# Last step of a two-layer graph kernel as seven half products on one Trainium2 core

## The chip, the core and the metric

The kernel runs on one core of one Trainium2 chip. The core has five engines that run side by side and meet at semaphores: TensorE (matrix products into PSUM; PE in the profile, with its weight loads as PEld), VectorE (DVE), ScalarE (ACT), GpSimd (POOL) and SyncE (SP), whose queue issues almost all transfers of this kernel, in order. The metric is the device time of the whole program in microseconds (us); lower is better. All data is float32.

## What is computed

There are 16 batches of 1024 nodes with 256 channels, and one adjacency matrix of 1024 x 1024 for all of them. Layer 0 is an attention over the nodes whose queries come from a product with a weighted adjacency; layer 1 is a graph convolution in two steps with a residual. Each layer ends in a LayerNorm over the 256 channels. The change concerns layer 1:

```python
def _graph_conv(x, adj, w_loop, w_neigh, b):
    loop = jnp.einsum('bnd,dh->bnh', x, w_loop)
    neigh = jnp.einsum('nm,bmh->bnh', adj, jnp.einsum('bnd,dh->bnh', x, w_neigh))
    return loop + neigh + b
h = jax.nn.relu(_graph_conv(x, adj, w1_loop, w1_neigh, b1))   # 256 -> 128
h = jax.nn.relu(_graph_conv(h, adj, w2_loop, w2_neigh, b2))   # 128 -> 256
return (x + h) * 0.5
...
x = _layernorm(x + _L1_gnn_ref(x, adj, ...), axis=-1)
```

With u = adj h1 (128 wide, one row per node), the second step ends in h2 = u w2_neigh + h1 w2_loop + b2. That is one product of [u, h1] (1024 x 256) with the two stacked weight matrices (256 x 256). Since LayerNorm undoes a common factor, the kernel scales w2 and b2 by 1/3 and adds relu(h2) to the layer's input x1 directly.

## The kernel before

**Batches overlap.** The loop over b in `run` works on four batches at once: the attention of batch b, the queries, keys and values of batch b + 1, the graph convolution's second half for batch b - 2 joined with the first half for batch b - 1, and the LayerNorm and output of batch b - 3. From batch 2 on, `c1`, `c2` and `c3` are the convolutions of b - 1, b - 2 and b - 3. The order in which the engines get their work is written out by hand (`tc.manual_schedule()`), so an engine does what the program issues for it, in the program's order, and each engine waits by itself for what it needs.

**One batch in order** (batches 2 to 14, the branch `elif more`):

- Scores of the first head pair (L692), exponentials on ScalarE (L697, L699), sums of the exponentials on VectorE (`collect`, L711 and L713, then the block transpose L718 and the reduction L721 in `partial`).
- Meanwhile the 256-channel sums of the next batch's x on ScalarE (`NodeSums`, L276), which write x in place.
- Products of exponentials and values (L734) for two units, each drained by a transpose on VectorE (L745); between them the transposes of the next x (L228).
- Sums for keys and values of the next batch (`KeysValues.sums`, L413 to L421, VectorE).
- `c1.inner()`: t = x1 w1_neigh (L847), copied by ScalarE (L850).
- `both.left(nc.gpsimd)`: four sums of blocks of t and h1 on GpSimd, the tiles R (L1052 to L1055).
- `both.run(...)`: the joined product with the adjacency, for t of batch b - 1 and h1 of batch b - 2 together: seven products of quarters instead of eight (Strassen-Winograd), issued as 1, 2, 6, 7, 5, 4, 3 (L1061), with the loop term of the first step (L854) at the start and ahead of product 3. It uses three PSUM banks called first, third and second, which ScalarE copies out (L1077, L1083, L1087, L1090). Its results are h1 of batch b - 1 (L860) and u of batch b - 2 (upper half on VectorE, L1094; lower half on GpSimd, L1095).
- Between the products other work is issued through the dictionary handed to `run`: the sums S of blocks of the next x for its queries (`q.left`, GpSimd, L596 to L599) after product 1; `att.add` (denominators by a small product L754, then L760 to L767 on VectorE) after product 2; `likeness` (two ScalarE activations, L550 and L551) and `c3.moments` (statistics L300 and L301 on VectorE, variance plus epsilon L305 there, power -1/2 on GpSimd L306) after product 6; `likeness` again after 7; `weigh_first` (L556, L609 to L612, VectorE) after 5; `c3.finish` (scaling L312 on VectorE and the output store L945 on SP) after 4.
- `c2.last()`: the last step of batch b - 2, 16 products 256 wide (L916 with w2_neigh, L918 with w2_loop) into two large PSUM tiles; for each tile VectorE adds b2 (L923), and then takes the maximum with 0 and adds x1 (L926).
- `c1.turn_blocks()` (L876 and stores of h1), scores and outputs of the second head pair, and `weigh_second`.
- The queries' seven products for the next batch, in four steps (`q.pair`, `q.step`, L637), `att.add` for the second pair, the mean and squares of the first LayerNorm, `q.load_para`, `kv.load` (weight sums kept in DRAM), loads of the next x in two layouts (L96, L108), then keys and values by seven products (L434 and L438), the variance with its power on GpSimd (L351), and the first LayerNorm's scaling (L356), transposes (L228) and stores (L364).

Batch 15 (the branch `else`) has no next batch: only `both.left`, `both.run` with `att.add` and the first LayerNorm woven in, `c1.turn(0)` (transposes on TensorE, L893), `c2.last()`, `c1.turn(1)`. After the loop come the convolutions that are left.

**Buffers.** Most tiles of 128 x 1024 come from one pool of 31 buffers (`row_tile`); a new tile waits for the last reader of the tile that had its buffer. PSUM has three large tiles ("big") and two single banks ("bank").

Of the kernel before, what the change touches and what calls it, by code (L numbers as in the profile page):

```python
# [10 lines left out]
F32 = mybir.dt.float32  # L11
# [7 lines left out]
def kernel(  # L19
# [108 lines left out]


    kv_sums = dram.tile([P, N], F32, tag="kv_sums", name="kv_sums", bufs=1)  # L130

    def sum_kv_weights():
        t = row_tile("kv_sums")
# [10 lines left out]
    def load_weights():  # L144
        nc.sync.dma_start(out=w1l_sb, in_=w1_loop.rearrange("(cc p) f -> p cc f", p=P))
        nc.sync.dma_start(out=w1n_sb, in_=w1_neigh.rearrange("(cc p) f -> p cc f", p=P))
        nc.sync.dma_start(out=w2l_sb, in_=w2_loop)
        nc.sync.dma_start(out=w2n_sb, in_=w2_neigh)
        nc.sync.dma_start(out=b1_sb, in_=b1.rearrange("(p o) -> p o", o=1))
        nc.sync.dma_start(out=b2_sb, in_=b2.rearrange("(o f) -> o f", o=1).to_broadcast([P, C]))  # L150

        for w in (w2l_sb, w2n_sb, b2_sb):
            nc.gpsimd.tensor_scalar_mul(w, w, 1.0 / 3.0)
        for w in (w1l_sb, w1n_sb):
            nc.gpsimd.tensor_scalar_mul(w, w, LIFT)

    ident = const.tile([P, P], F32, name="ident")
    make_identity(nc, ident)
# [164 lines left out]
    class BlockedNorm:  # L323
# [23 lines left out]
        def variance(self):  # L347
            self.rstd = small.tile([P, NB], F32, tag="rstd1", name=f"rstd1_{self.name}", bufs=2)
            nc.vector.tensor_scalar(self.rstd, fold_sums(self.part, f"sum2_{self.name}", half_psum), 1.0 / C, EPS,  # L349
                                    op0=ALU.mult, op1=ALU.add)  # L350
            nc.gpsimd.tensor_tensor(self.rstd, self.rstd, neg_half, ALU.pow)  # L351

# [479 lines left out]
    class GraphConv:  # L832
# [95 lines left out]
        def last(self):  # L928
# [6 lines left out]
                filled.append(p2)  # L935
            return filled

        def moments(self):
            self.mv = small.tile([P, NT, 2], F32, tag="mv", name=f"mv_{self.b}", bufs=2)
            statistics(self.mv, self.x, range(NT), f"g{self.b}")  # L940
            self.rstd = reciprocal_deviation(self.mv, f"g{self.b}", EPS2)

        def finish(self, dst):
# [86 lines left out]
    class Joined:  # L1030
# [24 lines left out]
            eng.tensor_sub(s34[:, 1], t1[1], s12[:, 1])  # L1055
            self.x = {1: t1[0], 2: t1[1], 3: s34[:, 1], 4: h1[1], 5: s12[:, 0], 6: s12[:, 1], 7: s34[:, 0]}

        def product(self, n, dst, start=False, again=False):
            rows = self.far[{1: "00", 2: "10", 3: "11", 4: 4, 5: 1, 6: 2, 7: 3}[n]]
            for k in range(TJ):  # L1060
                nc.tensor.matmul(dst, self.x[n][:, k, :], of_rows(rows, k),  # L1061
                                 start=(start and k == 0), stop=(k == TJ - 1), skip_group_check=again)

        def run(self, between=None):
            c1, c2, b = self.c1, self.c2, self.b
            between = between or {}

            def turn_to(n):
                for f in between.get(n, ()):
# [9 lines left out]
            self.product(2, third)  # L1079
            nc.vector.tensor_add(p1, p1, third)  # L1080
            turn_to(2)
            self.product(6, first, again=True)
            nc.scalar.copy(u1, first)  # L1083
            c1.relu(0, p1)
# [9 lines left out]
            nc.vector.tensor_add(c2.uT[:, 0:FB], u1, second)  # L1094
            nc.gpsimd.tensor_add(c2.uT[:, FB:N], u3, p7)  # L1095
            turn_to(4)
            c1.loop(first, 1, again=True)
            self.product(3, first, again=True)
            c1.relu(1, first)
            turn_to(3)  # L1100

    def run():
# [58 lines left out]
        for b in range(B):  # L1161
# [72 lines left out]
            elif more:  # L1234
# [10 lines left out]
                    ready["xT"] = channel_major(blocked, f"xT_{b + 1}")  # L1245

                two_units(0, before_second=next_xT)
                kv = KeysValues(b + 1, ready["xT"])
                kv.sums()
                both.fetch(2, 3)  # L1250
# [3 lines left out]
                for t in (0, TJ):  # L1254
# [13 lines left out]
                order = (1, TJ + 1, 2, TJ + 2, 3, TJ + 3)  # L1268
# [54 lines left out]
            elif more:  # L1323
                q.pair(2)
                q.step(0)
                q.step(1, lambda: att.add(*((2, 3) if both else (3,))), 5)
                q.pair(3)
                q.step(2, norm.mean)
# [12 lines left out]
            else:  # L1341
# [96 lines left out]
```

## Time and profile before

| what | value |
|---|---|
| median of three runs | 2139.09 us (2138.91 to 2139.37) |
| the profiled execution's own time | 2138.39 us |
| its span, first to last instruction | 2136.6 us |
| granted TensorE clock | 0.998 |
| one batch in the middle, t_ps to t_ps | 131.5 us |
| last step in such a batch, L916 and L918 | 6.9 us |
| VectorE, ScalarE, GpSimd busy | 89%, 49%, 16% |
| transfers | 341 MB, 159 GB/s over the span from HBM and to it |

In the timeline each row has the start in the span, the duration, the engine, the line, the operation, output and input with their shapes, and how many instructions were merged; in brackets stands how long the engine was idle before it, and what released it. The chain of waits lists start, duration, engine and line. A float32 product shows as two records, each with its own weight load. Durations on TensorE overlap, since products are pipelined; the distance from one start to the next is what a product costs.

### The profile page before, as it was taken

The page shows a single profiled execution, that of the slowest core. Times are in us where ns is not written, and L with a number is a line of the kernel's source. Part 1 is how long each engine was busy: PE and PEld are TensorE (multiplying, and loading weights), DVE is VectorE, ACT ScalarE, POOL GpSimd, SP SyncE. Part 2 cuts the span into 40 slices and gives each one's busy share as a digit, 9 for nine tenths or more (in the row PEclk, how much of TensorE's full clock was granted, in tenths as well). Part 3 has the DMA queues.
Part 4 walks back from the last instruction along what each step waited for, and adds up shares of the span by engine and source line. Part 5 has one row for each costly group of instructions (what it writes and reads, how often), then busy time and mean ns, then how long its engine had stood idle before and what let it go on. Part 6 is the DMA issues. An engine that isn't in the chain of part 4 may idle for free.

```text
span 2136.6 us, 24125 instructions
## 1 busy us (share of the span) xinstructions
PE 2124.6 (99%) x8374; PEld 1028.2 (48%) x8374; DVE 1896.7 (89%) x2373; ACT 1048.5 (49%) x1498; POOL 345.7 (16%) x191
## 2 busy tenths in 40 slices
PE   9999999999999999999999999999999999999998
PEld 5344544544445455454454444544445444544454
DVE  6899988989898898988989989899998999989964
ACT  5745545555355462545625555355554445545412
POOL 1010120121302113030130301303012130121021
PEclk9999999999999999999999999999999999999999
DMA  9295666736676275763747638466473666734544
GB/s 236 98 171 196 133 214 145 187 121 119 216 156 218 82 137 197 158 217 105 145 168 153 217 122 154 149 148 217 132 178 124 138 217 146 181 117 97 162 158 157
DMA packets 611409, 341.09 MB, mean 160 GB/s; under 512 B 491728, under 2 KB 556624, under 8 KB 611280
## 3 DMA queue, kind: packets, MB, share of 16 engines
q1 hardware_dynamic: 611008, 339.21, 60.9%
q8 instruction: 68, 1.11, 0.2%
q14 instruction: 61, 0.50, 0.1%
q10 hardware_dynamic: 272, 0.26, 0.0%
HBM read 289.54 MB, written 49.87 MB: 159 GB/s over the span
## 4 chain that ended last, share of the span: by engine, by line
PE 98%; DVE 1%; issue 0%; ACT 0%; POOL 0%; POOLq 0%; DVEq 0%
PE s L692 21%; PE av L734 20%; PE hu_ps L1061 17%; PE g_ps L637 15%; PE v_ps L438 5%; PE k_ps L434 5%; PE t_ps L847 3%; PE g_ps L564 3%; PE h_ps L916 2%; PE h_ps L918 2%; PE hu_ps L854 2%; PE h_ps L869 1%; PE u_ps L898 1%; PE den_ps L754 0%; DVE wg L556 0%
## 5 line engine op out<-in xcount | busy, mean ns | idle before, releaser
L713 DVE TENSOR_TENSOR acc<-acc,pr 128x1024 f32<-128x1024 f32 x384 | 473.2, 1232 | 36.7 <-DVE acc L713 0.9
L699 ACT ACTIVATE pr<-s 128x1024 f32<-128x1024 f32 x392 | 390.7, 1115 | 142.2 <-PE s L692 142.2
L692 PE MATMUL s<-qT,kT 64*128 64x512 f32 x2048 | 449.7, 593 | 0.0
L734 PE MATMUL av<-pr,v 128*64 128x512 f32 x2048 | 447.0, 594 | 0.0
L692 PEld LDWEIGHTS s<-qT,kT 64*128 64x128 f32 x2048 | 196.3, 187 | 235.5 <-issue 187.3
L734 PEld LDWEIGHTS av<-pr,v 128*64 128x64 f32 x2048 | 144.0, 137 | 297.3 <-issue 272.6
L351 POOL TENSOR_TENSOR rstd<-rstd,neg_half 128x32 f32<-128x32 f32 x16 | 100.2, 6260 | 1116.1 <-DVE rstd L349 1116.1
L1061 PE MATMUL hu_ps<-adj,R 128*128 128x512 f32 x480 | 211.8, 594 | 0.0
L550 ACT ACTIVATE wg<-c_row,c_sums 128x1024 f32<-128x1024 f32 x120 | 137.1, 1142 | 86.5 <-DVE den_part L721 65.8
L556 DVE SCALAR_TENSOR_TENSOR wg<-wg,adj 128x1024 f32<-128x1024 f32 x128 | 150.1, 1210 | 5.0 <-ACT wg L551 5.0
L697 ACT ACTIVATE pr<-s 128x512 f32<-128x512 f32 x240 | 142.4, 702 | 0.3 <-PE s L692 0.3
L1061 PEld LDWEIGHTS hu_ps<-adj,R 128*128 128x128 f32 x480 | 90.1, 190 | 108.1 <-issue 105.0
L551 ACT ACTIVATE wg<-wg 128x1024 f32<-128x1024 f32 x128 | 135.3, 1057 | 4.1
L637 PE MATMUL g_ps<-T,S 128*128 128x512 f32 x224 | 116.5, 602 | 0.2 <-DVE T L611 0.2
L637 PE MATMUL g_ps<-wg,S 128*128 128x512 f32 x224 | 115.5, 597 | 0.0
L850 ACT COPY t<-t_ps 128x1024 f32<-128x1024 f32 x16 | 16.2, 1013 | 189.4 <-PE t_ps L847 189.4
L637 PE MATMUL g_ps<-wg,x 128*128 128x512 f32 x224 | 109.0, 599 | 0.0
L1061 PE MATMUL hu_ps<-adj,t 128*128 128x512 f32 x240 | 105.7, 592 | 0.0
L646 ACT COPY P<-g_ps 128x512 f32<-128x512 f32 x14 | 8.2, 586 | 183.9 <-PE g_ps L637 106.6
L923 DVE TENSOR_TENSOR z<-h_ps,b_sb 128x1024 f32<-128x1024 f32 x30 | 36.7, 1224 | 59.4 <-PE h_ps L918 59.4
L1052 POOL TENSOR_TENSOR R<-h 128x512 f32<-128x512 f32 x14 | 28.2, 2012 | 358.2 <-DMA adj<-adjT 241.5
L711 DVE TENSOR_TENSOR acc<-pr,pr 128x1024 f32<-128x1024 f32 x64 | 76.9, 1201 | 6.2 <-ACT pr L699 6.2
(210 smaller groups left out, 3131.3 us busy)
## 6 DMA issues: line engine op xcount, KB each, us to landing
adj<-adjT SPq DMA_DIRECT2D x210, 512.0 KB
adj<-in_adj_dram SPq DMA_DIRECT2D x128, 512.0 KB
para<-in_L_gnn_para_dram SPq DMA_DIRECT2D x32, 512.0 KB
xB_a<-in_x_dram SPq DMA_DIRECT2D x128, 128.0 KB
x1d<-xB_a SPq DMA_DIRECT2D x128, 128.0 KB
x<-x1d SPq DMA_DIRECT2D x16, 1024.0 KB
xB<-in_x_dram SPq DMA_DIRECT2D x120, 128.0 KB
x<-in_x_dram SPq DMA_DIRECT2D x15, 1024.0 KB
```

What stands on the lines that cost most here:

```text
L434: nc.tensor.matmul(dst, self.a[0][n], self.w[n], start=not again, stop=True, skip_group_check=again)
L438: nc.tensor.matmul(dst[:, ts(t, P)], self.w[n][:, ts(t, P)], self.a[1][n], start=not again and t == 0, stop=True, skip_group_check=again o ...
L550: nc.scalar.activation(wg, self.c_row, AF.Abs, bias=self.c_col[:, t:t + 1], scale=-1.0)
L551: nc.scalar.activation(wg, wg, AF.Tanh, scale=-0.5 / C)
L556: nc.vector.scalar_tensor_tensor(wg, wg, 1.0, self.adj.pop(t), op0=ALU.add, op1=ALU.mult)
L637: nc.tensor.matmul(self.p[n], x_n[:, k, :], w_n, start=(k == 0), stop=(k == TJ - 1))
L692: nc.tensor.matmul(halves[s], self.kT[rows, pair, ts(mt, P)], self.qT[rows, pair, ts(j, FB)], start=True, stop=True)
L697: nc.scalar.activation(pr[:, ts(s, FB)], halves[s], AF.Exp)
L699: nc.scalar.activation(pr, ps, AF.Exp)
L713: nc.vector.tensor_add(self.acc, self.acc, prs[mt])
L734: nc.tensor.matmul(pav[s * HD:(s + 1) * HD, :], self.v[:, mt, pair * P + s * HD:pair * P + (s + 1) * HD], prs[mt][:, ts(s, FB)], start=(mt ...
L1061: nc.tensor.matmul(dst, self.x[n][:, k, :], of_rows(rows, k), start=(start and k == 0), stop=(k == TJ - 1), skip_group_check=again)
```

## The change

The last step of batch b - 2 is written as seven products of 128 x 128 blocks: [u, h1] is cut into u and h1 by columns and into upper and lower half by rows, the stacked weights into four 128 x 128 blocks. Sums of the weight blocks and the difference of the two halves of b2 are made once, on GpSimd, and kept in DRAM. In each batch they are fetched into a row buffer, and sums of blocks of u and h1 are made (one on GpSimd, three on VectorE). ScalarE writes the bias into two of the joined product's banks before the new products add to them. The joined product's product 3 is cut in two: the order on TensorE is loop term, half of product 3, parts 1, 2, 6, 5, 7, the other half of product 3, parts 4 and 3. This holds for batches 2 to 15 of the loop; the convolutions after the loop keep the old last step.

Beside that, the work woven in between the joined products is placed anew. `q.left` (S) and the statistics of batch b - 3 now stand ahead of the keys' and values' sums; the two `likeness` calls, `att.add`, the deviation and `weigh_first` stand after products 1 and 2. The last LayerNorm's scaling goes to ScalarE (`finish_aside`, as it was used after the loop before), after step 0 of the queries' products, and its store to the same place. In batch 15 the variance uses a single bank, and the first LayerNorm's scaling and transposes stand after the new block sums.

```diff
+    w2_sums = dram.tile([P, 5 * P], F32, tag="w2_sums", name="w2_sums", bufs=1)
@@ load_weights
+        t = row_tile("w2_sums")
+        (b11, b12), (b21, b22) = ((w[:, ts(0, P)], w[:, ts(1, P)]) for w in (w2n_sb, w2l_sb))
+        t1, t2, t3, t4, b2_step = (t[:, ts(n, P)] for n in range(5))
+        nc.gpsimd.tensor_sub(t1, b12, b11)
...
+        nc.gpsimd.tensor_sub(b2_step, b2_sb[:, ts(1, P)], b2_sb[:, ts(0, P)])
+        nc.sync.dma_start(out=w2_sums, in_=t[:, 0:5 * P])
@@ GraphConv
+        def load_sums(self):
+            self.w2 = row_tile(f"w2_sums_{self.b}")
+            nc.sync.dma_start(out=self.w2[:, 0:5 * P], in_=w2_sums)
+            self.b2_step = self.w2[:, ts(4, P)]
+
+        def block_sums(self, base, lower):
...
+            lower()
+            nc.gpsimd.tensor_add(s1, self.h1T[:, FB:N], self.low)
+            base()
+            nc.vector.tensor_sub(s2, s1, self.up)
+            nc.vector.tensor_sub(s4, self.h1T[:, 0:FB], s2)
+            nc.vector.tensor_sub(s3, self.up, self.low)
...
+        def seventh_part(self, n, dst, start=False):
+            a, w = self.factors[n]
+            for t in range(TJ):
+                first = start and t == 0
+                nc.tensor.matmul(dst[:, ts(t, P)], a[:, ts(t, P)], w, start=first, stop=True, skip_group_check=not first)
+
+        def settle(self, i, j, src):
+            rows = self.x[:, ts(i, TJ), ts(j, P)]
+            nc.vector.scalar_tensor_tensor(rows, src.rearrange("p (t c) -> p t c", c=P), 0.0, rows,
+                                           op0=ALU.max, op1=ALU.add)
+
+        def last_products(self, a, c):
...
+            self.seventh_part(1, a)
+            nc.scalar.copy(p1, a)
+            self.seventh_part(2, d, start=True)
+            nc.vector.tensor_add(p1, p1, d)
+            self.settle(0, 0, p1)
+            self.seventh_part(6, a)
+            nc.scalar.copy(u2, a)
+            self.seventh_part(5, c)
+            self.seventh_part(7, a)
+            nc.scalar.copy(u3, a)
+            nc.vector.tensor_add(u3, u3, c)
+            self.settle(1, 1, u3)
+
+            def rest():
+                self.seventh_part(4, a)
+                self.settle(1, 0, a)
+                self.seventh_part(3, c)
+                nc.vector.tensor_add(u2, u2, c)
+                self.settle(0, 1, u2)
...
@@ Joined.run
             turn_to(2)
+            if last:
+                bias(third, b2_sb[:, ts(0, P)])
+                c2.load_sums()
...
+            c2.block_sums(add_upper, add_lower)
+            bias(second, c2.b2_step)
             turn_to(4)
             c1.loop(first, 1, again=True)
-            self.product(3, first, again=True)
+            self.product(3, first, again=True, steps=range(0, TJ // 2))
+            rest = c2.last_products(third, second)
+            self.product(3, first, again=True, steps=range(TJ // 2, TJ))
             c1.relu(1, first)
+            rest()
@@ run, batches 2 to 14
                 two_units(0, before_second=next_xT)
+                q.left(nc.gpsimd)
+                if c3:
+                    c3.statistics()
                 kv = KeysValues(b + 1, ready["xT"])
                 kv.sums()
...
-                both.run({1: (lambda: q.left(nc.gpsimd),),
-                          2: (lambda: att.add(0, 1),),
-                          6: (lambda: q.likeness(0), lambda: c3 and c3.moments()),
-                          7: (lambda: q.likeness(TJ),),
-                          5: (weigh_first,),
-                          4: (lambda: c3 and c3.finish(out[b - 3]),)})
-                c2.last()
+                both.run({1: (lambda: q.likeness(0),),
+                          2: (lambda: att.add(0, 1), lambda: q.likeness(TJ), lambda: c3 and c3.deviation(), weigh_first)},
+                         last=True)
...
                 q.step(0)
+                if c3:
+                    c3.finish_aside(out[b - 3])
                 q.step(1, lambda: att.add(*((2, 3) if both else (3,))), 5)
@@ run, batch 15
-                          5: (norm.variance,), 4: (norm.scale, norm.spread)})
+                          5: (lambda: norm.variance(bank_psum),), 4: (norm.scale, norm.spread)}, last=True)
                 c1.turn(0)
-                c2.last()
                 c1.turn(1)
```

More of the change, by code (lines that the diff above doesn't have):

```diff
@@ L155, in load_weights @@
             nc.gpsimd.tensor_scalar_mul(w, w, LIFT)
+        t = row_tile("w2_sums")
+        (b11, b12), (b21, b22) = ((w[:, ts(0, P)], w[:, ts(1, P)]) for w in (w2n_sb, w2l_sb))
+        t1, t2, t3, t4, b2_step = (t[:, ts(n, P)] for n in range(5))
+        nc.gpsimd.tensor_sub(t1, b12, b11)
+        nc.gpsimd.tensor_sub(t2, b22, t1)
+        nc.gpsimd.tensor_sub(t3, b22, b12)
+        nc.gpsimd.tensor_sub(t4, b21, t2)
+        nc.gpsimd.tensor_sub(b2_step, b2_sb[:, ts(1, P)], b2_sb[:, ts(0, P)])
+        nc.sync.dma_start(out=w2_sums, in_=t[:, 0:5 * P])
     ident = const.tile([P, P], F32, name="ident")
@@ L345, in sum_squares, with variance @@
             join(self.part)
-        def variance(self):
+        def variance(self, psum_tile=half_psum):
             self.rstd = small.tile([P, NB], F32, tag="rstd1", name=f"rstd1_{self.name}", bufs=2)
-            nc.vector.tensor_scalar(self.rstd, fold_sums(self.part, f"sum2_{self.name}", half_psum), 1.0 / C, EPS,
+            nc.vector.tensor_scalar(self.rstd, fold_sums(self.part, f"sum2_{self.name}", psum_tile), 1.0 / C, EPS,
                                     op0=ALU.mult, op1=ALU.add)
@@ L936, in last @@
             return filled
+        def load_sums(self):
[3 more added lines that the diff above has]
+        def block_sums(self, base, lower):
+            s12, s34 = (row_tile(f"last_{self.b}_{k}") for k in range(2))
+            self.low, self.up = self.uT[:, FB:N], self.uT[:, 0:FB]
+            s1, s2, s3, s4 = s12[:, 0:FB], s12[:, FB:N], s34[:, 0:FB], s34[:, FB:N]
+            lower()
[4 more added lines that the diff above has]
+            nc.vector.tensor_sub(s3, self.up, self.low)
+            t1, t2, t3, t4 = (self.w2[:, ts(n, P)] for n in range(4))
+            self.factors = {1: (self.up, w2n_sb[:, ts(0, P)]), 2: (self.h1T[:, 0:FB], w2l_sb[:, ts(0, P)]),
+                            3: (s4, w2l_sb[:, ts(1, P)]), 4: (self.h1T[:, FB:N], t4), 5: (s1, t1), 6: (s2, t2), 7: (s3, t3)}
@@ new lines, in last_products @@
+        def last_products(self, a, c):
+            name = f"h2_{self.b}"
+            d = bank_psum(f"{name}_ps")
+            snaps = [row_tile(f"{name}_{k}") for k in range(2)]
+            p1, u2, u3 = snaps[0][:, 0:FB], snaps[0][:, FB:N], snaps[1][:, 0:FB]
+            self.seventh_part(1, a)
[16 more added lines that the diff above has]
+                self.settle(0, 1, u2)
+            return rest
@@ L938, in moments, with statistics, deviation @@
         def moments(self):
+            self.statistics()
+            self.deviation()
+        def statistics(self):
             self.mv = small.tile([P, NT, 2], F32, tag="mv", name=f"mv_{self.b}", bufs=2)
             statistics(self.mv, self.x, range(NT), f"g{self.b}")
+        def deviation(self):
             self.rstd = reciprocal_deviation(self.mv, f"g{self.b}", EPS2)
@@ L1056, in left, with product, run, bias @@
             self.x = {1: t1[0], 2: t1[1], 3: s34[:, 1], 4: h1[1], 5: s12[:, 0], 6: s12[:, 1], 7: s34[:, 0]}
-        def product(self, n, dst, start=False, again=False):
+        def product(self, n, dst, start=False, again=False, steps=range(TJ)):
             rows = self.far[{1: "00", 2: "10", 3: "11", 4: 4, 5: 1, 6: 2, 7: 3}[n]]
-            for k in range(TJ):
+            for k in steps:
                 nc.tensor.matmul(dst, self.x[n][:, k, :], of_rows(rows, k),
                                  start=(start and k == 0), stop=(k == TJ - 1), skip_group_check=again)
-        def run(self, between=None):
+        def run(self, between=None, last=False):
             c1, c2, b = self.c1, self.c2, self.b
             between = between or {}
+            def bias(bank, row):
+                nc.scalar.copy(bank.rearrange("p (t c) -> p t c", c=P), row.unsqueeze(1).to_broadcast([P, TJ, P]))
             def turn_to(n):
@@ L1093, in run @@
             c2.uT = row_tile(f"uT_{c2.b}")
-            nc.vector.tensor_add(c2.uT[:, 0:FB], u1, second)
-            nc.gpsimd.tensor_add(c2.uT[:, FB:N], u3, p7)
+            add_upper = lambda: nc.vector.tensor_add(c2.uT[:, 0:FB], u1, second)
+            add_lower = lambda: nc.gpsimd.tensor_add(c2.uT[:, FB:N], u3, p7)
+            if not last:
+                add_upper()
+                add_lower()
+                turn_to(4)
+                c1.loop(first, 1, again=True)
+                self.product(3, first, again=True)
+                c1.relu(1, first)
+                turn_to(3)
+                return
+            c2.block_sums(add_upper, add_lower)
+            bias(second, c2.b2_step)
             turn_to(4)
             c1.loop(first, 1, again=True)
-            self.product(3, first, again=True)
+            self.product(3, first, again=True, steps=range(0, TJ // 2))
+            rest = c2.last_products(third, second)
+            self.product(3, first, again=True, steps=range(TJ // 2, TJ))
             c1.relu(1, first)
+            rest()
             turn_to(3)
```

## The prediction

> **What bounds the kernel now.** I read the page first. TensorE is busy 99% of the span and holds 98% of the chain that ended last, so the time is TensorE's list of products plus every moment at which that list waits.
>
> ```profile
> PE 2124.6 (99%) x8374; PEld 1028.2 (48%) x8374; DVE 1896.7 (89%) x2373; ACT 1048.5 (49%) x1498; POOL 345.7 (16%) x191
> PE 98%; DVE 1%; issue 0%; ACT 0%; POOL 0%; POOLq 0%; DVEq 0%
> ```
>
> Batches 3 to 14 repeat every 131.5 us (t_ps starts at 1077.05, and 131.48 later again); I work in the one from 1049 to 1181 us. In the chain, in order of time, stand the last step (its 32 records, L916 and L918, from 1108.51) and the pattern that the change copies, products of halves (L434 and L438):
>
> ```profile
> 1105.08 3.43 PE hu_ps L1061 x8
> 1108.51 0.43 PE h_ps L916 x2
> 1108.94 0.43 PE h_ps L918 x2
> ...
> 1171.65 0.86 PE k_ps L434 x2
> 1172.51 0.89 PE v_ps L438 x8
> 1173.40 0.91 PE k_ps L434 x2
> 1174.31 0.92 PE v_ps L438 x8
> ```
>
> The reader sees no gap: whatever is to be saved must come out of TensorE's own products, and whatever comes late elsewhere is paid only when TensorE waits. The timeline of the engines around 1074 shows what feeds the next products (L1061), and how VectorE and GpSimd get on:
>
> ```profile
> 1068.08 2.55 DVE L713 TENSOR_TENSOR acc<-acc,pr 128x1024 f32<-128x1024 f32 x2
> 1068.12 0.36 ACT L276 ACTIVATION_READ_ACCUMULATOR x<-x 128x1 f32 x1
> 1070.68 5.00 DVE L713 TENSOR_TENSOR acc<-acc,pr 128x1024 f32<-128x1024 f32 x4
> 1074.71 2.10 POOL L1052 TENSOR_TENSOR R<-h 128x512 f32<-128x512 f32 x1 [24.16 <-DMA adj<-adjT]
> 1076.99 1.22 DVE L721 TENSOR_REDUCE den_part<-accB 128x32 f32<-128x1024 f32 x1
> 1078.13 0.71 DVE L745 STREAM_TRANSPOSE o<-av 128x512 f32<-128x512 f32 x1
> 1080.86 1.01 ACT L850 COPY t<-t_ps 128x1024 f32<-128x1024 f32 x1 [12.37 <-PE t_ps L847]
> 1081.95 0.19 PEld L1061 LDWEIGHTS hu_ps<-adj,t 128*128 128x128 f32 x1 [0.24 <-ACT t L850]
> ...
> 1083.35 1.71 POOL L1054 TENSOR_TENSOR R<-t,h 128x512 f32<-128x512 f32 x1
> 1083.86 1.75 DVE L420 TENSOR_TENSOR K<-xT 128x512 f32<-128x512 f32 x1
> 1085.02 1.71 POOL L1055 TENSOR_TENSOR R<-t,R 128x512 f32<-128x512 f32 x1
> ...
> 417.40 2.27 DVE L713 TENSOR_TENSOR acc<-acc,pr 128x1024 f32<-128x1024 f32 x1
> ```
>
> VectorE works through from 1068 without a pause, and two of its results stand just ahead of TensorE. The other thing to see: a VectorE operation with two inputs in SBUF and a GpSimd operation take turns. L420 takes 0.68 alone and 1.75 here, with GpSimd's L1054 and L1055 around it; the one L713 that GpSimd got ahead of took 2.27 instead of 1.22. So one turn costs VectorE 1.05 to 1.07 us.
>
> **The change, part by part** (lines of the kernel before; us per batch, times as in the batch shown).
>
> *Products.* Removed: 16 products 256 wide, 32 records at 0.2155, 6.90. Added: 28 products 128 wide. The same shape in the same alternation is L438: 0.89 for four, so 28 cost 6.23. By the dearer row, t_ps (3.77 for 16), they cost 6.60. I take -0.68, the pattern's own row; the bounds are -0.31 and -0.68.
>
> *Turnarounds.* Parts 6 and 7 go onto a bank that ScalarE has just copied, behind one group of 0.89. Where L438 does this (1173.40 to 1176.32) groups take 0.91, 0.92 and 0.94 instead of 0.86, 0.89 and 0.86: I take +0.1 (0 to 0.2). Cover: ScalarE, idle 8.0 before L860; the two bias copies (0.58 each) and three drains go there.
>
> *VectorE's sums.* Gone: two L923 and two L926 (4 x 1.22) and eight L312 (2.67). New: ten 512-wide operations at 0.69 and a shift of 0.2. The load hardly moves; its place does. After the last product stand 0.69 + 0.69 + 1.24 (L876) instead of 1.22 + 1.22 + 1.24, and the adds L711 wait for the second L699 instead, 3.05 after the scores begin against 3.6 now. The second half's chain, which ends in T of step 3, thus comes 0.4 earlier; the 56 records of L637 there take 24.6 for 24.05 of pure work, so I take -0.3 (0 to -0.5).
>
> *S sums of the next batch (L596 to L599) moved ahead of the R sums (L1052).* This is the step that decides. In the changed program they wait only for the last L276 (1068.48), so GpSimd starts them at 1068.6, in the middle of the six L713. Four S operations and L1052 then take turns with the last five adds: 5 x 1.06 = 5.3. Queued behind the adds on VectorE are L718, L721 and L745. L721 ends at 1078.21 now, 1083.5 then. In the changed program the copy L850 goes into the buffer that L721 reads last, and the first product L1061 goes into the bank that L745 drains. Slack: L850 starts at 1080.86, 2.65 after L721's end. The copy runs 1083.5 to 1084.5, the load of weights goes from 1081.95 to 1084.6, and L1061 begins at 1084.8 instead of 1082.54: a stall of 2.3. Bounds: 0 (if no more than two turns are lost, 2.1, below the slack) and 3.1 (if each turn costs GpSimd's contended 1.71 less the 0.5 that it waited itself). I take 2.3, since L420 and the 2.27 row are this very pairing.
>
> [...]
>
> *Statistics (L300, 4.36) moved ahead of K sums (L413 to L421).* They no longer meet GpSimd there, which saves three turns. VectorE reaches L1080 at 1078.21 + 5.3 + 3.8 (L745, L228, L745) + 4.36 + 2.6 = 1094.3; the product before it ends at 1091.8 with the stall. Late by 2.5, but only ScalarE's bias copy and relu(0) wait for it. Then 5.5 to the end of L767, 5.0 for L556 to L612 with two more turns (the lower uT and the new sum s1 on GpSimd): uT's upper half at 1107.8. TensorE, after L854 and half of product 3, wants it at 1109.2. Cost nothing; if the 1.4 of cover are gone, each us late is one per batch.
>
> *LayerNorm on ScalarE, output stored later.* ScalarE is idle from 1151 to 1163.9; eight L952 (0.5 apart) follow the shift and end near 1159 with the shift of the batch. The store now stands in SP's queue ahead of para, kv_sums and the blocked x, which were issued from 1141.6 on. At 1 MB in 3.2 us (the store of before: 213 GB/s over 5 us at 63% busy), store, para and kv_sums land at about 1168; TensorE wants kv_sums at 1173. Nothing, with 4 to 5 us of cover; gone, each us costs one in 12 batches. Fetching w2_sums (0.3 MB) comes after 1090, when the transfer engines show 0.00 busy: nothing.
>
> *Batch 15.* No S sums there. But s2 waits for GpSimd: L351 to 2055.88, then two sums of 1.26, to 2058.4. Behind s2, s4, s3 (to 2060.5) on VectorE stand the scaling L356 and the transposes L228 (4.7), then p1, a settle and u3 (2.1): 2067.3. The last product of the seven waits for u3; then two groups of turns. t_ps starts near 2069.5 instead of 2066.58: +2.9 net (-0.7 if VectorE kept up, +4).
>
> *Start.* The store of w2_sums holds SP from 41.3 to about 50; x of batch 1 is wanted at 64.2: nothing.
>
> **Sum.** Batches 2 to 14: -0.68 + 0.1 - 0.3 + 2.3 = +1.42, times 13 is +18.5; batch 15 +2.9. The profiled execution took 2138.39 (span 2136.6 and 1.8 around it): 2159.8. The median shown is 0.7 above it: 2160.
>
> **Rivals.**
> 1. *The turns are absorbed* and the saved products remain. For it: the 2.27 of one batch left its L850 where it was, and 2.65 us of slack. Against it: five turns, not one. It decides if no more than two and a half turns (2.65 / 1.06) are lost. Then 13 x -0.88 + 2.9: 2130.6; with -0.7 in batch 15, 2127.
> 2. *Near balance*: about three or four turns (stall 0.2 to 1.2): 13 x (-0.7 to +0.3) + 2.9, 2133 to 2146, of which a part lies within 0.2%.
> 3. *SP's queue becomes the wait*: the store lands late, kv_sums arrives after 1173. For it: one queue in order, eight transfers open. Against it: 4 us. With 1 us lost beyond the cover in 12 batches on top of the forecast: 2172; two: 2184.
> 4. *The product saving is not there*: 128-wide at t_ps's 0.2356: 13 x 0.37 more, 2165, still the forecast's side.
>
> **How the numbers follow.** What a measurement of this kernel can tell from no change is about 0.2%, 4.3 us. The forecast (with rival 4) has 0.66 and its own range 2150 to 2168; rival 1 0.21; rival 2 0.07, of which 0.05 within 0.2%; rival 3 0.06. Faster 0.22, same 0.05, slower 0.73. The likeliest gives 2160. The range has to reach into rival 1 to leave out no more than 2 in 10: 2129 to 2168.
>
> **What would show it.** In the changed trace: L713 rows of 2.2 to 2.3 beside GpSimd's S sums near 1068 to 1079 of a batch; L850's copy released by VectorE's L721 (not by TensorE) and a gap of about 2 us on TensorE before the first L1061; t_ps to t_ps 132.9 instead of 131.48; the seven products in 6.2 to 6.4 and no wait at them; kv_sums' load ahead of its products. Wrong would be: adds of 1.22 throughout, L1061 following L854 without a gap, a period under 131.

## The result, and the profile after

The changed kernel takes 2157.93 us (median of four runs, 2155.34 to 2158.99) against 2139.14 us for the kernel before on the same chip (2138.91 to 2139.37): ratio 1.0086, 95% interval 1.0069 to 1.0104. It is slower by 18.8 us; 2160 was forecast. The profiled execution took 2157.34 us and spans 2155.6 us, 19.0 more than the one before.

In what follows, lines up to about L937 have numbers 10 higher than in the kernel before: the adds are L721 and L723, the block transpose L728, the reduction L731, the bank's drain L755, the copy of t L860, the S sums L606 to L609. The R sums are L1125 to L1128, the joined products L1134, the seven products L971.

The page of the changed kernel, busy times and the chain that ended last:

```profile
PE 2121.1 (98%) x8710; PEld 1035.5 (48%) x8710; DVE 1898.0 (88%) x2373; ACT 1138.2 (53%) x1664; POOL 391.8 (18%) x210
PE 27%; DVE 7%; POOL 2%; issue 1%; ACT 0%; DMA 0%; SPq 0%; DVEq 0%; POOLq 0%; ACTq 0%
```

TensorE is busy 3.5 us less than before and yet the program is longer: TensorE has got waits. The chain could be followed back only as far as 1326 us, so its shares add up to 37% of the span; in this part VectorE and GpSimd stand in it, where before TensorE held 98% of the whole. GpSimd has 19 operations more and 46 us more of busy time: 24 us are the new sums, and the S sums take 30 us longer than before, the R sums 8 us less. What TensorE waits for (view of the waits: in total, times, longest):

```profile
PE hu_ps L1134 <- ACT t L860: 21.5, 13, 3.5
PE hu_ps L971 <- DVE h L993: 2.2, 1, 2.2
```

There are thirteen waits for the copy of t, one in each of the batches 2 to 14, and one in batch 15 for an add of VectorE (L993). The timeline around one of them, the batch whose t_ps starts at 1087.73 us (start, duration, engine, line, operation; in brackets the idle time before and what ended it):

```profile
1078.83 3.44 DVE L723 TENSOR_TENSOR acc<-acc,pr 128x1024 f32<-128x1024 f32 x2
1079.31 1.87 POOL L606 TENSOR_TENSOR S<-x 128x512 f32<-128x512 f32 x1 [18.01 <-ACT x L286]
...
1081.26 2.14 POOL L607 TENSOR_TENSOR S<-S,x 128x512 f32<-128x512 f32 x1
...
1082.32 8.80 DVE L723 TENSOR_TENSOR acc<-acc,pr 128x1024 f32<-128x1024 f32 x4
...
1083.36 2.25 POOL L608 TENSOR_TENSOR S<-x 128x512 f32<-128x512 f32 x1
...
1085.57 2.25 POOL L609 TENSOR_TENSOR S<-x,S 128x512 f32<-128x512 f32 x1
...
1087.78 2.25 POOL L1125 TENSOR_TENSOR R<-h 128x512 f32<-128x512 f32 x1
...
1092.43 1.22 DVE L731 TENSOR_REDUCE den_part<-accB 128x32 f32<-128x1024 f32 x1
1093.57 0.71 DVE L755 STREAM_TRANSPOSE o<-av 128x512 f32<-128x512 f32 x1
1093.76 1.01 ACT L860 COPY t<-t_ps 128x1024 f32<-128x1024 f32 x1 [14.53 <-DVE den_part L731]
1094.19 2.33 DVE L238 STREAM_TRANSPOSE xT<-xB 128x1024 f32<-128x1024 f32 x2
1094.82 0.30 PEld L1134 LDWEIGHTS hu_ps<-adj,t 128*128 128x128 f32 x2 [2.37 <-ACT t L860]
```

Read it from the top: four adds take 8.80 us instead of 5.00, 2.20 each, as long as one GpSimd operation lasts beside them (2.25). VectorE's reduction therefore ends 5.92 us after the start of t_ps, 1.23 before; the copy of t waits for it, and TensorE's weights wait for the copy. The one-input operations further down (L728 and L731, 1.25 and 1.22, and L238) are as fast as ever.

The seven products behind it are in their place without a wait (start, duration, line):

```profile
1119.18 1.05 PE L971 MATMUL hu_ps<-w2n_sb,uT 128*128 128x128 f32 x8
1120.08 1.06 PE L971 MATMUL h_ps<-w2l_sb,h1T 128*128 128x128 f32 x8
1120.97 2.99 PE L971 MATMUL hu_ps<-w_sums,last 128*128 128x128 f32 x24
1123.80 1.88 PE L1134 MATMUL hu_ps<-adj,R 128*128 128x512 f32 x4
1125.52 1.05 PE L971 MATMUL hu_ps<-w_sums,h1T 128*128 128x128 f32 x8
1126.41 1.06 PE L971 MATMUL hu_ps<-w2l_sb,last 128*128 128x128 f32 x8
1127.39 14.00 PE L702 MATMUL s<-qT,kT 64*128 64x512 f32 x64
```

Start to start, they take 4.62 + 1.87 = 6.49 us, against 7.00 for the old last step (1108.35 to 1115.35). One middle batch in three stretches:

| from, to | before | after | difference |
|---|---|---|---|
| start of t_ps, first joined product | 5.40 | 7.09 | +1.69 |
| first joined product, scores | 32.97 | 32.57 | -0.40 |
| scores, next t_ps | 93.11 | 92.88 | -0.23 |
| sum | 131.48 | 132.54 | +1.06 |

Two small differences belong to the way in which a wait shows. The idle time of 1.54 is less than the 1.69 by which the first product is late, since the end of one product otherwise overlaps the start of the next (by 0.16 in the kernel before, where L854 ends at 1082.54 and L1061 starts at 1082.38). And the sixteen records behind the wait take 6.97 us from start to start instead of 6.87, which is why the second row has -0.40 where the seven products alone gain 0.51.

And the whole span, by the starts of t_ps: up to batch 2 +0.53, batch 2 alone +4.71 (136.18 instead of 131.47), the other twelve together +12.51, batch 15 +2.54 (42.09 instead of 39.55), the rest -1.33, in all 18.95. The -1.33 is at the very end, where the code is the same: the last store is issued 0.4 earlier behind VectorE's last operation and ends 4.4 us after its issue instead of 5.4; in the profiles of this study this stretch takes 68.6 to 70.2 us. The +0.53 at the start is no part of the change either: t_ps of the first batch starts between 173.2 and 174.5 us in the profiles of this study, without an order in it.

Batch 2 is another matter. Here are the reduction and the wait of this batch (t_ps starts at 288.65), and the granted clock after it (stretches of the changed kernel: bounds, length, busy time of each engine, then the clock, the transfer share and GB/s):

```profile
295.38 1.22 DVE L731 TENSOR_REDUCE den_part<-accB 128x32 f32<-128x1024 f32 x1
...
297.75 8.77 PE L1134 MATMUL hu_ps<-adj,t 128*128 128x512 f32 x16 [3.54 <-ACT t L860]
```

```profile
297.70:300.00 2.30, 2.25 (x3) 1.17 (x4) 2.30 (x4) 0.00 (x0) 2.16 (x2) 0.50 1.02 411
300.00:303.00 3.00, 3.00 (x7) 1.17 (x6) 2.97 (x4) 0.00 (x0) 2.01 (x2) 0.82 1.03 421
303.00:306.00 3.00, 3.00 (x9) 1.33 (x8) 0.76 (x2) 2.79 (x4) 0.00 (x0) 1.00 0.18 56
```

TensorE waited 3.54 us here instead of 1.54, and was then granted half its clock for a while: the sixteen records that take 7.03 without a wait (e1) took 8.77. The clock is 0.50 in the first row; 0.82 over the 3.00 us of the second means half the clock for 1.1 of them, so it came back at 301.1, 3.3 us after TensorE had gone on. How long a wait has to be for this, the traces do not settle (last section).

### The profile page after: what moved, and what is told of

The parts are those of the page before. It is cut to its first block, busy times and chain, and to the rows that moved or that the text cites. A ratio compares the mean times of both kernels' runs of the same rounds, so it can differ in the third digit from the quotient of the medians.

```text
span 2155.6 us, 25079 instructions
## 1 busy us (share of the span) xinstructions
PE 2121.1 (98%) x8710; PEld 1035.5 (48%) x8710; DVE 1898.0 (88%) x2373; ACT 1138.2 (53%) x1664; POOL 391.8 (18%) x210
## 5 line engine op out<-in xcount | busy, mean ns | idle before, releaser
L723 DVE TENSOR_TENSOR acc<-acc,pr 128x1024 f32<-128x1024 f32 x384 | 531.1, 1383 | 37.4 <-DVE acc L723 1.4
L1134 PE MATMUL hu_ps<-adj,R 128*128 128x512 f32 x480 | 214.2, 594 | 0.0
L1134 PEld LDWEIGHTS hu_ps<-adj,R 128*128 128x128 f32 x480 | 89.1, 190 | 101.4 <-issue 98.3
L860 ACT COPY t<-t_ps 128x1024 f32<-128x1024 f32 x16 | 16.2, 1012 | 219.1 <-DVE den_part L731 190.3
L1134 PE MATMUL hu_ps<-adj,t 128*128 128x512 f32 x240 | 108.7, 605 | 21.5 <-ACT t L860 21.5
L721 DVE TENSOR_TENSOR acc<-pr,pr 128x1024 f32<-128x1024 f32 x64 | 78.4, 1225 | 12.3 <-ACT pr L709 12.3
L1134 PEld LDWEIGHTS hu_ps<-adj,t 128*128 128x128 f32 x240 | 45.1, 193 | 84.0 <-issue 46.7
L728 DVE STREAM_TRANSPOSE accB<-acc 128x1024 f32<-128x1024 f32 x64 | 79.7, 1245 | 2.2
L731 DVE TENSOR_REDUCE den_part<-accB 128x32 f32<-128x1024 f32 x64 | 78.1, 1220 | 2.2
```

The source lines that it names most:

```text
L723: nc.vector.tensor_add(self.acc, self.acc, prs[mt])
L728: nc.vector.transpose(accB, self.acc)
```

## The experiments

Each is a kernel of its own; the ratio is against the kernel before on the same chip.

| run | what it is | us | ratio, 95% interval |
|---|---|---|---|
| e1_sums_back | changed, S sums back behind the R sums | 2132.5 | 0.9970 (0.9958 to 0.9982) |
| e2_sums_ahead_only | before, S sums ahead | 2166.7 | 1.0134 (1.0118 to 1.0149) |
| e3_batch2_back | changed, S sums back in batch 2 alone | 2153.0 | 1.0068 (1.0054 to 1.0081) |
| e4_buffer_early | changed, t1's buffer free earlier | 2152.9 | 1.0067 (1.0053 to 1.0080) |
| e5_two_ahead | changed, two of four S sums ahead | 2131.4 | 0.9965 (0.9952 to 0.9979) |
| e6_back_last15 | e1, old last step in batch 15 | 2128.1 | 0.9950 (0.9937 to 0.9964) |
| e7_back_sums15 | e1, batch 15's two sums on VectorE | 2127.6 | 0.9947 (0.9934 to 0.9961) |
| e8_back_old_last | e1, old last step in all batches | 2140.2 | 1.0007 (0.9998 to 1.0016) |
| e9_sums_on_vector | e7, S sums ahead on VectorE | 2137.7 | 0.9996 (0.9987 to 1.0005) |
| e10_finish_old | e7, last LayerNorm back on VectorE | 2127.0 | 0.9949 (0.9935 to 0.9963) |
| e11_statistics_old | e7, statistics later | 2147.1 | 1.0041 (1.0027 to 1.0055) |

### Is it the S sums? (e1, e2)

```diff
-                q.left(nc.gpsimd)
                 if c3:
                     c3.statistics()
...
-                both.run({1: (lambda: q.likeness(0),),
+                both.run({1: (lambda: q.left(nc.gpsimd), lambda: q.likeness(0)),
```

> The changed kernel with the S sums of the next batch back behind the R sums on GpSimd; all else as changed. Theory (the S sums take turns with VectorE's adds, and VectorE is late for the first product): in the middle batch the gap ahead of the first L1134 (1.54, and 1.70 against the kernel before from t_ps on) is gone, the 0.41 and 0.22 won behind it stay, so a period of 132.54 - 1.70 = 130.8 to 130.9 from t_ps to t_ps, the 4.7 of batch 2 goes too, batch 15 stays 2.5 dearer: 2139.1 - 13 x 0.65 + 2.5 + 0.5 = 2134 (2131 to 2137). Rival (the stall comes from the other moves, the seven products, the statistics or the copies on ScalarE): within 3 us of the changed kernel, 2155 to 2160. Rival (the S sums there take turns with the K sums and make uT late): period 131.5 or more, 2139 to 2148.

e2 does the opposite in the kernel before:

```diff
                 two_units(0, before_second=next_xT)
+                q.left(nc.gpsimd)
                 kv = KeysValues(b + 1, ready["xT"])
...
-                both.run({1: (lambda: q.left(nc.gpsimd),),
-                          2: (lambda: att.add(0, 1),),
+                both.run({2: (lambda: att.add(0, 1),),
```

> The kernel before with nothing changed but the S sums, issued ahead of the R sums as in the changed kernel. Theory: the adds take 2.2 each beside them, the first L1061 begins 1.6 to 1.8 later in twelve batches and 4 to 5 in batch 2, and nothing is won behind it: 2139.1 + 12 x 1.7 + 4.5 = 2164 (2159 to 2167), slower than the changed kernel, since the seven products and the earlier second half win 0.6 a batch there. Rival (the S sums cost nothing by themselves): 2137 to 2141.

Measured 2132.5 and 2166.7, both inside what the theory gave. In e1 the period is 130.74, batch 2 included, and the timeline of a batch whose t_ps starts at 1073.30 shows why:

```profile
1067.01 4.99 DVE L723 TENSOR_TENSOR acc<-acc,pr 128x1024 f32<-128x1024 f32 x4
...
1073.31 1.22 DVE L731 TENSOR_REDUCE den_part<-accB 128x32 f32<-128x1024 f32 x1
...
1077.18 1.01 ACT L860 COPY t<-t_ps 128x1024 f32<-128x1024 f32 x1 [12.37 <-PE t_ps L857]
...
1078.69 7.03 PE L1134 MATMUL hu_ps<-adj,t 128*128 128x512 f32 x16
...
1083.36 1.60 POOL L607 TENSOR_TENSOR S<-S,x 128x512 f32<-128x512 f32 x1
1083.87 1.65 DVE L424 TENSOR_TENSOR K<-xT,K 128x512 f32<-128x512 f32 x1
```

The adds are back at 1.25, the copy waits for TensorE alone, and no gap stands ahead of L1134. The turns have not vanished: the S sums now meet the K sums (L424 takes 1.65), but nothing that TensorE wants soon is queued behind these. So the early S sums alone cost 28 us (e2), and taking them out of the change turns its loss into a gain of 6 us.

### Why batch 2 costs more (e3)

The S sums stand ahead only where there is a c3, that is from batch 3 on.

```diff
-                q.left(nc.gpsimd)
                 if c3:
+                    q.left(nc.gpsimd)
                     c3.statistics()
...
-                both.run({1: (lambda: q.likeness(0),),
+                both.run({1: (lambda: c3 or q.left(nc.gpsimd), lambda: q.likeness(0)),
```

> The changed kernel with the S sums back behind the R sums in batch 2 alone. Theory (in batch 2 VectorE is already some 3 us later against t_ps than in the other batches, so the same turns cost a stall of 3.54, and after it TensorE is granted 0.50 of its clock for a while, 1.7 more): t_ps of batch 2 to the next falls from 136.18 to about 130.9, the time to 2157.9 - 5.2 = 2152.7 (2151 to 2155); the first sixteen L1134 of that batch take 7.0 instead of 8.77. Rival (batch 2 loses by the seven products or the first fetches instead): 135 to 136 as now, 2156 to 2159.

Measured 2153.0; batch 2 takes 130.74 and the waits are twelve, 1.5 each. In the kernel before, the trace of batch 2 had the reduction L721 end 4.24 us after the start of t_ps, not 1.23 as in the batch that the prediction worked in:

```profile
283.88 5.94 DVE L713 TENSOR_TENSOR acc<-acc,pr 128x1024 f32<-128x1024 f32 x4
...
285.76 1.72 POOL L1052 TENSOR_TENSOR R<-h 128x512 f32<-128x512 f32 x1 [24.05 <-DMA adj<-adjT]
...
288.12 3.84 PE L847 MATMUL t_ps<-w1n_sb,x1T 128*128 128x128 f32 x32
...
291.14 1.22 DVE L721 TENSOR_REDUCE den_part<-accB 128x32 f32<-128x1024 f32 x1
```

One turn, that of the first R sum, is in these rows already (5.94 for four adds). In the changed kernel the four of the S sums come on top, and the reduction ends 7.95 after t_ps, 3.71 later than before. By as much the first joined product is late; the fall of the clock adds 1.74, the rest of the batch saves 0.74, and that is the 4.71.

### Buffer or bank (e4)

```diff
                 q.left(nc.gpsimd)
+                c1.t1 = row_tile(f"t1_{c1.b}")
+                nc.scalar.copy(c1.t1[:, 0:1], b1_sb)
```

The small copy takes a buffer early that TensorE has left, and the copy of t1 writes into the same tile.

> The changed kernel with the buffer of the t1 copy (L860) taken earlier, so that the copy waits for TensorE alone and no longer for VectorE's L731; the S sums stay ahead and the first L1134 still waits for the bank that L755 drains. Theory (VectorE is late, and the bank is the second wait): the adds still take 2.2 each, the copy ends long before, L1134 begins 0.1 behind L755's end, some 0.45 earlier than now: 2157.9 - 13 x 0.45 = 2152 (2150 to 2155). Rival (the buffer alone is the cause, since moving the allocation is what made the copy wait): the gap goes, 2131 to 2137.

Measured 2152.9, period 132.05. From e4's timeline, t_ps starting at 1084.29:

```profile
1088.21 1.01 ACT L860 COPY t<-t_ps 128x1024 f32<-128x1024 f32 x1 [12.35 <-PE t_ps L857]
...
1090.11 0.71 DVE L755 STREAM_TRANSPOSE o<-av 128x512 f32<-128x512 f32 x1
...
1090.92 7.11 PE L1134 MATMUL hu_ps<-adj,t 128*128 128x512 f32 x16 [1.07 <-issue]
```

The copy is done at 1089.2, and TensorE still waits until the drain of its bank ends at 1090.82. (The profile puts this wait to "issue", since it does not name the drain; the start 0.1 behind the drain's end does.) So there are two waits, one for the buffer and one for the bank; in the changed kernel the drain of the bank ended 0.5 us before the copy (1094.28 and 1094.77), and what is late behind both is VectorE. Of the 6.2 us that batches 2 to 14 gain in e4, batch 15 takes back 1.5 (43.61 instead of 42.09): the clock fell behind its wait, as the last section tells.

### How many turns are free (e5)

`left` is cut in two, the first two sums ahead of the R sums, the other two behind them. (From there on lines are 4 higher in this kernel.)

```diff
-                q.left(nc.gpsimd)
+                q.left(nc.gpsimd, False)
...
-                both.run({1: (lambda: q.likeness(0),),
+                both.run({1: (lambda: q.left_rest(nc.gpsimd), lambda: q.likeness(0)),
```

> The changed kernel with only the first two of the four S sums ahead of the R sums, the other two behind them; all else as changed. Theory (turns are lost one by one, and nothing is paid until VectorE's slack is gone): three GpSimd operations, two S sums and the first R sum, meet the adds instead of five, VectorE is 2 to 3 us later instead of 4.8, and the bank that L755 drains has some 3.4 us of slack in the batches 3 to 14, so no gap there and a period of 130.7 to 130.8; in batch 2, where L755 ended 0.5 ahead of the first product in the kernel before, a gap of 1.5 to 2.5. Time 2132.5 + 1.5 to 4 = 2134 to 2137. Rival (each S sum ahead costs its share): halfway between the changed kernel and the one with the sums back, 2144 to 2147.

Measured 2131.4, a little below what was expected. The middle batch has no gap (5.39 from t_ps to the first joined product, period 130.74), and batch 2 only 0.3 of one, where 1.5 to 2.5 was expected: only two operations met the adds, not three, because the first R sum was held back itself.

```profile
1068.46 5.94 DVE L727 TENSOR_TENSOR acc<-acc,pr 128x1024 f32<-128x1024 f32 x4
...
1077.06 1.27 POOL L1129 TENSOR_TENSOR R<-h 128x512 f32<-128x512 f32 x1 [7.53 <-DVE den_part L735]
```

Four adds take 5.94, 0.95 more than alone, for the second of the two turns. Two turns make VectorE 1.8 us late at the reduction and are free, five make it 4.7 late and cost 1.7 a batch: the loss has a threshold, it is not a share for each sum, as the rival had it. Three and four turns were not tried.

### Batch 15 (e6, e7)

e6 has the old last step there (and the half-size tile for the variance again):

```diff
-                          ... 4: (norm.scale, norm.spread)}, last=True)
+                          ... 4: (norm.scale, norm.spread)})
                 c1.turn(0)
+                c2.last()
                 c1.turn(1)
```

> The changed kernel with the S sums back behind the R sums, and in batch 15 the last step of the kernel before (32 products 256 wide, added in one piece); batches 2 to 14 as changed. Theory (s2 behind GpSimd's power and two sums, and the scaling and the transposes ahead of the add that frees the bank, cost a wait of 2.2 and one of 0.4): t_ps of batch 15 to the last t_ps back from 42.7 to 39.5, the time 2132.5 - 3.2 = 2129.3 (2128 to 2131). Rival (batch 15 is dearer by the moved variance or the fetches): 2132 to 2134.

e7 keeps the seven products and changes the engine of two sums there:

```diff
-            nc.gpsimd.tensor_add(s1, self.h1T[:, FB:N], self.low)
+            eng.tensor_add(s1, self.h1T[:, FB:N], self.low)
...
-            add_lower = lambda: nc.gpsimd.tensor_add(c2.uT[:, FB:N], u3, p7)
+            add_lower = lambda: eng.tensor_add(c2.uT[:, FB:N], u3, p7)
...
-                          5: (lambda: norm.variance(bank_psum),), 4: (norm.scale, norm.spread)}, last=True)
+                          5: (lambda: norm.variance(bank_psum),), 4: (norm.scale, norm.spread)}, last=True, eng=nc.vector)
```

> The changed kernel with the S sums back behind the R sums, and in batch 15 the lower half of uT and the sum s1 on VectorE instead of GpSimd, which is at its power there; seven products in all batches. Theory (it is GpSimd that s2 waits for): s4 and s3 are done some 3 us earlier, the add that frees the bank ends before the last product wants it or 0.3 behind, both waits of batch 15 are gone: 2132.5 - 2.6 to 3.4 = 2129.5 (2128 to 2131). Rival (it is VectorE's own list, the scaling and the transposes ahead of that add, that is late): the wait stays above 1.5, 2131.5 to 2134.

Measured 2128.1 and 2127.6, the second a little below its range. Batch 15 takes 39.55 with the old step and 39.09 with the seven products once both waits are gone. In the changed kernel it had gone like this:

```profile
2068.19 5.44 POOL L361 TENSOR_TENSOR rstd<-rstd,neg_half 128x32 f32<-128x32 f32 x1 [14.59 <-DVE rstd L359]
...
2074.93 1.27 POOL L958 TENSOR_TENSOR last<-h1T,uT 128x512 f32<-128x512 f32 x1
...
2076.24 0.69 DVE L960 TENSOR_TENSOR last<-last,uT 128x512 f32<-128x512 f32 x1 [4.12 <-POOL last L958]
...
2080.45 2.37 DVE L238 STREAM_TRANSPOSE x1T<-xB_a 128x1024 f32<-128x1024 f32 x2
...
2084.03 0.68 DVE L993 TENSOR_TENSOR h<-h,hu_ps 128x512 f32<-128x512 f32 x1
...
2084.76 1.16 PE L971 MATMUL hu_ps<-w2l_sb,last 128*128 128x128 f32 x8 [2.16 <-DVE h L993]
```

GpSimd is at its power, VectorE idles 4.12 us for the sum behind it, does the scaling and the transposes next, and the add that frees the bank comes 2.16 too late. e7 has the seven products in every batch and the S sums where the kernel before had them; it is 11 us ahead of the kernel before and 30 ahead of the changed one.

### What the seven products are worth (e8)

e1 with `c2.last()` as before in all batches (batch 15 as in e6); the statistics and the LayerNorm stay as changed.

```diff
-                         last=True)
+                )
+                c2.last()
                 c1.turn_blocks()
```

> The changed kernel with the S sums back behind the R sums and the last step of the kernel before in all batches; the statistics earlier and the LayerNorm on ScalarE as changed. Theory (the seven products win 0.5 a batch on TensorE, and VectorE's second half begins earlier because the last add behind them is half as wide): from the first L1134 to the scores 32.97 as in the kernel before instead of 32.47, from the scores to t_ps 93.1 as before instead of 92.9, period 131.5, time 2139 (2138 to 2140). Rival (the gain of the second half comes from the LayerNorm that left VectorE): 92.9 stays, period 131.25, 2135 to 2137.

Measured 2140.2, at the upper edge of the theory's range. In its profile the stretch from the first joined product to the scores is 32.97 again (32.47 in e1), and from the scores to t_ps 93.19 (92.88 in e1). Both gains come with the seven products; without them the rest of the change gains nothing that these runs can tell from zero.

### Contention or place (e9)

```diff
                 two_units(0, before_second=next_xT)
+                q.left(nc.vector)
                 if c3:
                     c3.statistics()
...
-                both.run({1: (lambda: q.left(nc.gpsimd), lambda: q.likeness(0)),
+                both.run({1: (lambda: q.likeness(0),),
```

> The kernel with the S sums back and batch 15's two sums on VectorE (2127.6), but with the S sums where the change puts them in the order, on VectorE instead of GpSimd. Theory (the loss came from the two engines taking turns, not from the place or the buffers): the adds take 1.22 to 1.24 throughout, the four S sums cost VectorE 2.8 behind the transposes and the four K sums fall from 6.9 (beside GpSimd) to 2.7, the copy L860 follows t_ps without a wait, no gap: 2127.6 within 1.5. Rival (the early place, or the t1 buffer that it brings, is what costs): gaps of 1 us or more, 2140 to 2158.

Measured 2137.7: the theory was half right. The adds take 1.24, and there is no gap ahead of L1134. But in their new place the S sums meet GpSimd's R sums, and TensorE has a new wait (timeline of e9, and its waits of TensorE):

```profile
1082.89 1.64 DVE L607 TENSOR_TENSOR S<-S,x 128x512 f32<-128x512 f32 x1
1083.95 1.71 POOL L1127 TENSOR_TENSOR R<-t,h 128x512 f32<-128x512 f32 x1
1084.45 1.75 DVE L608 TENSOR_TENSOR S<-x 128x512 f32<-128x512 f32 x1
```

```profile
PE hu_ps L971 <- DVE uT L1173: 6.5, 12, 0.8
```

Three of the four S sums take 1.64 to 1.75 instead of the 0.69 that was reckoned, the statistics come later by that, and uT's upper half is 0.5 late for the first of the seven products in each of twelve batches. With the overlap that such a wait breaks (0.16) and slower first products behind it (0.1), that is the 0.75 between a period of 131.49 and 130.74.

### LayerNorm and statistics (e10, e11)

e10 puts `c3.finish` back among the calls after product 4; e11 puts the statistics where the deviation stands.

```diff
@@ e10
-                          2: (..., lambda: c3 and c3.deviation(), weigh_first)},
+                          2: (..., lambda: c3 and c3.deviation(), weigh_first),
+                          4: (lambda: c3 and c3.finish(out[b - 3]),)},
...
-                if c3:
-                    c3.finish_aside(out[b - 3])
@@ e11
-                if c3:
-                    c3.statistics()
...
-                          2: (..., lambda: c3 and c3.deviation(), weigh_first)},
+                          2: (..., lambda: c3 and c3.moments(), weigh_first)},
```

> The same kernel (2127.6) with the LayerNorm's last step back on VectorE, eight operations of 0.33 in the place where the kernel before had them, and the store issued there. Theory (it was hidden on either engine): 2.7 us more on VectorE between the block sums and the add of part 2, where 0.8 and 2.0 us are idle, so the last add is no later and the period stays 130.74: 2127.6 within 1.5. Rival (VectorE is short there, and the move to ScalarE is part of the gain): the add that frees a bank comes late, a wait before a product of the seven, 0.3 to 1.5 a batch, 2131 to 2147.

> The same kernel (2127.6) with the LayerNorm's statistics (4.4 us of VectorE) later, behind the second product's add and the first half's sums instead of ahead of the K sums. Theory (the place costs nothing): the K sums meet GpSimd's R and S sums as now, and uT's upper half is ready when it is now, 0.9 ahead of the first of the seven products: 2127.6 within 2. Rival (the early place keeps VectorE off GpSimd's sums and is needed): uT late by 1 us or more beyond that 0.9, a wait before the first of the seven products in 12 batches, 2135 or more.

Measured 2127.0 and 2147.1. The LayerNorm's engine and the store's place make no difference. The statistics' place does, by 19.5 us, against what was expected. The waits of TensorE in e11:

```profile
PE hu_ps L971 <- DVE uT L1173: 16.6, 12, 1.5
```

```profile
1093.83 0.69 DVE L1156 TENSOR_TENSOR snap<-snap,hu_ps 128x512 f32<-128x512 f32 x1 [2.23 <-PE hu_ps L1134]
```

With the statistics later, VectorE idles 2.2 us ahead of the second product's add (L1156) and has the 4.4 us of statistics to do between that add and uT. Ahead of the K sums they fill that idle time, beside GpSimd, whose operations do not slow them (0.38 to 0.42 each in either place). Fewer turns are not what is gained: up to uT the two-input operations on VectorE lose about as much in e7 (the K sums take 6.9 beside the S sums instead of 2.7) as in e11 (the K sums 5.8 beside the R sums, and L776 1.64 instead of 0.69).

## Why the prediction was right, point by point

- **The S sums ahead of the R sums.** The step that was to decide did: the mechanism, the copy released by the reduction, the bank as the second wait, and the gap. Its size was too large: one turn costs VectorE 0.95 (8.80 less 5.00, over four), not 1.06; five cost 4.7 at the reduction (5.92 less 1.23), not 5.3; the gap is 1.69, not 2.3. VectorE's one-input operations lost nothing beside GpSimd: L728 took 1.25 beside an R sum in e1 and 1.25 without one in the changed kernel, L731 1.22 beside one in e4 and 1.22 without one in the changed kernel, the statistics 0.38 to 0.42 each in either place (e11).
- **Times 13.** This term failed: the batch was taken to stand for all of them. Batch 2 cost 4.71 instead of 1.42, because VectorE ran 3 us later there already and the clock fell at the longer gap (e3). The twelve others cost 12.5 instead of 17.0; the two errors nearly cancel, 17.2 against 18.5. That the total came within 2 us of the forecast is in part luck.
- **Products and turnarounds, -0.58.** (By its own rows, 6.90 less 6.23, the first term is 0.67, not 0.68, and the other bound 0.30, not 0.31; it makes no difference.) Measured -0.51 (6.49 against 7.00), the pattern's own row held; parts 6, 5 and 7 took 2.83 for three groups instead of 2.67, a little more than the 0.1 put down for turnarounds.
- **Second half, -0.3.** The adds begin 3.15 after the scores instead of 3.67, so 0.5 earlier; 3.05 and 3.6 were forecast, which is 0.55 and not the 0.4 that the text made of it. Measured -0.23, and e8 shows that it comes with the seven products.
- **Statistics, nothing.** Right in the change: the K sums no longer meet GpSimd (0.66 to 0.69 each), and uT's upper half is ready 2.5 us before TensorE wants it, where 1.4 was forecast. But "nothing" hides that the place is needed once the S sums are back: 1.65 a batch without it (e11).
- **LayerNorm and the store, nothing.** Right (e10). In the changed kernel the store is issued at 1169.15 and the weight sums at 1171.48, and the products that read these start at 1183.30, without a wait.
- **Batch 15, +2.9.** Measured +2.54, by the steps named: s2 behind GpSimd's power and two sums, then the scaling and transposes, then the add (e7).
- **Rivals.** That the turns are absorbed is true of two of them (e5), as its threshold of two and a half said; with five it is not. The queue of transfers was no wait, and the saving of the products was there.

## What to carry to other kernels

A sum on GpSimd is not free because GpSimd is idle: look which two-input operations VectorE does in that time, count one turn for each (0.95 us of VectorE here), and compare with the slack of what is queued behind them; below the slack it cost nothing here, above it all of the rest. VectorE's one-input work ran beside GpSimd's sums without loss (statistics 0.38 to 0.42, transposes 1.25, reductions 1.22, with a sum beside them or without), so it can stand there; where VectorE waits for a product is a good place for it (e11). Before a per-batch price is multiplied, look at the slack in the first and the last batch too, since the same delay costs more where the engine is already late (batch 2 took 4.71 us longer, each of the twelve others 1.04).

## What had not been expected of the hardware

A wait of TensorE can cost more than its length. In batch 2 of the changed kernel, with a wait of 3.54 us, the granted clock fell to 0.50, and 1.7 us more were lost; with the twelve waits of 1.08 to 1.54 in the batches 3 to 14 it stayed at 1.00. Above these the length alone does not decide. In batch 15 the changed kernel waited 0.42 and then 2.16 and kept the clock at 1.00; e1, with the same two waits, fell to one half (rows below), and so did e4 (43.61 for the batch; its mean granted clock is 0.997, that of the changed kernel and of e1 0.998). e4 fell in batch 2 as well: behind a wait of 3.11 the sixteen records took 8.50, not the 7.13 that they take behind a wait of 1.54. In e1 the fall came only 1.1 us after TensorE had gone on; in batch 2 of e2 the sixteen records behind a wait of 3.53 took 8.83. In the changed kernel the stretch at half the clock lasted 3.41 us (297.70 to 301.11). The one in e1 (bounds, length, busy time, clock, transfers, from the end of the wait on):

```profile
2058.20:2060.00 1.80, 1.80 (x13) 1.80 (x14) 1.80 (x3) 0.00 (x0) 0.00 (x0) 0.81 0.96 139
2060.00:2062.00 2.00, 2.00 (x11) 2.00 (x10) 1.16 (x3) 1.17 (x2) 0.00 (x0) 0.50 0.98 144
```

e1 lost 0.6 by it (42.71 against 42.09 for batch 15), e4 1.5. What decides between falling and not falling is open. This may be why kernels with such waits scatter more from run to run (e1 from 2129.96 to 2134.92, the kernel before within 0.6 on the same chip): of the changed kernel's four runs the shortest, 2155.34, has a mean granted clock of 0.999, the two longest, 2158.51 and 2158.99, have 0.997. It was not tried by itself.
